# Layer 0 of a two-layer graph and expert kernel: chains of the third graph block over 12 groups, GpSimd's indirect DMAs in program order, first weights issued earlier

## The chip, the cores and the metric

The kernel runs on one core of one Trainium2 chip. Its time is the device time in microseconds of one execution; lower is better. Before the change three runs took 1025.27, 1031.23 and 1034.23 us (median 1031.23). Besides, one execution was recorded by the hardware profiler.

Engines are named as in the profile: PE (matrix multiply), PEld (its weight loads), DVE (vector), ACT (scalar, activation functions), POOL (GpSimd) and SP (here a queue that only issues DMAs). Every engine runs its own instructions in order. DMAs are issued by SP, by ACT and by POOL; an indirect DMA, which takes row numbers from a tile, is issued by POOL alone.

## The reference

Two layers, each a graph step and a mixture of experts, on 3327 rows of 256 numbers. The change is in layer 0:

```python
def _L0_gnn_ref(x, adj, W, b):
    a = (adj == 1).astype(x.dtype)
    deg = jnp.sum(a, axis=1, keepdims=True)
    agg = jnp.einsum('ij,jf->if', a, x) / deg
    return agg @ W.T + b

def _L0_ffn_ref(x, gate_w, gate_b, w1, w2, w3):            # 16 experts, hidden size 512
    logits = jnp.einsum('bsd,de->bse', x, gate_w) + gate_b
    probs = jax.nn.softmax(logits, axis=-1)
    top_probs, top_idx = jax.lax.top_k(probs, 2)
    ...
    hidden = jax.nn.silu(h1) * h2
    expert_out = jnp.einsum('bseh,eho->bseo', hidden, w3)
    return jnp.einsum('bseo,bse->bso', expert_out, dispatch)

x = x + _L0_gnn_ref(_layernorm(x, axis=-1), adj, L0_gnn_W, L0_gnn_b)
x = x + _L0_ffn_ref((_layernorm(x, axis=-1))[None], ...)[0]
```

Layer 1 is of the same build: attention over the graph, then two of six experts for each row.

## The kernel before

**Tiles and chunks.** The rows stand in 26 tiles of 128 (the last has 127). Four tiles make a chunk, 0 to 6; chunk 6 has two tiles.

**Graph step (`graph`).** The result rows are worked in three blocks: block 0 has chunks 0 to 2, block 1 chunk 3, block 2 chunks 4 to 6. In a block the matmuls (L797) run over groups of source tiles. For each group SP loads a piece of the transposed adjacency matrix (`load_adj`, L669 and, for the last rows, L672), DVE turns it into a mask (`mask_of`, L680 and L682), and PE multiplies. Adjacency tiles and masks have three buffers each (`AHEAD`). Block 0 and block 2 have 26 groups of one tile, block 1 has ten of up to three tiles. A group of block 2 is twelve matmuls.

**The chain of a chunk (`finish`).** When a block's sums are there, each of its chunks goes through a chain that is written as a generator of seven steps: the first two tiles' product with W (L740) and update of x (L743, L858); the other two; layer norm (`norm`, L263 to L275) with stores of x and of the normed rows to DRAM; transposes for the router (L757); logits (L825, L827); the first part of `dispatch`, which finds the two experts of each row up to the tile `took` (L297 to L327); the second part, which counts places with matmuls (L333 to L337), casts them to row numbers (`t_idx`, L359) and writes (row, source row, weight) into the experts' lists in DRAM: eight indirect DMAs a chunk, issued by POOL (L363). The chains of a block run beside the next block's groups, two chunks in turn. `left` counts the steps that remain, and `over` gives the number of groups over which they are spread: after a group of block b, `left` over (`over[b]` less the group's number) steps are taken, rounded up.

**Expert slots (`slots0`).** A slot is up to 256 places of one expert's list; 32 usual ones (0 to 31) are run, the first eight from the lists of chunks 0 to 3 alone. Slot s: SP loads its piece of the list (`places0`, tile `who`, L952); POOL gathers the normed rows by two indirect DMAs (`rows_in0`, tile `xg`, three buffers, L1002); PE transposes them (L1015); two halves of the hidden layer (`hidden0`, L1027, with L1031 on ACT and L1035 on DVE); the product with w3 (`out0`, L1050); the weighting on DVE (tile `y`, two buffers, L1055); and two indirect DMAs on POOL that add the rows to x in DRAM (L1056). The weights of an expert come by three loads on SP (`load0`, L978): w1 and w2 by `load0_hidden`, w3 by `load0_out`, into two sets of buffers. The texts call the DMAs of L1002 gather s, those of L1056 add s, and those of L363 list scatters.

**How they meet.** In block 2 `routed0` runs at group 21 and loads `who` for slots 0 to 7; it reads the lists and so waits until the scatters of chunks 0 to 3 have landed. At group 25 the first step of `slots0` runs (gathers 0 and 1, slot 0's weights and transposes). After the block, `beside` takes two steps of the chains of chunks 4 to 6 for each half slot. From slot 8 on, the places of a slot come from `rank_table` and the lists of all chunks.

**What sets the order.** A scheduler orders the instructions of each engine by what is ready, except where the program ties them: `tc.issue_after(x)` keeps an instruction behind x on its engine's queue. SP's loads of slots are tied by `in_order` and `last["who"]`; POOL's indirect DMAs of the slots are not tied to each other. `add_manual_dep` makes a real wait: in block 2's chunks each list scatter waits until the one two before it has landed.

Of the kernel before, what the change touches and what calls it, by code (L numbers as in the profile page):

```python
# [15 lines left out]
OP = mybir.AluOpType  # L16
# [3 lines left out]
P = 128  # L20
# [5 lines left out]
def kernel(  # L26
# [26 lines left out]
    nc = tc.nc  # L53
# [6 lines left out]
    NP = NT * P  # L60
# [35 lines left out]
    GRAPH0 = [CHUNKS[:3], CHUNKS[3:4], CHUNKS[4:]]  # L96
    NE0 = sum(map(len, CHUNKS[:4]))
    assert NE0 <= NF and len(GRAPH0[2]) <= 3
    SA = 2 * P
    HALF = E0 // 2  # L100
    WIDTHS = [SA, SA - 32, SA - 32, SA - 64, SA - 64, SA - 64, SA - 96, SA - 96]
    assert len(WIDTHS) == HALF and NP % SA == 0
    USUAL0 = 4 * HALF
# [14 lines left out]
    hd = dram.tile([NP, D], F32, name="hd")  # L118
# [4 lines left out]
    hd_of = dram_disjoint_views(hd[:, :], 2)  # L123
    xd = dram.tile([NP + SA, D], F32, name="xd")
    xd_of = dram_disjoint_views(xd[:, :], 5)
# [49 lines left out]
    for i in range(2):  # L175
        where = const.tile([P, NT, 2, 3], I32, name=f"where{i}")
# [64 lines left out]
    last = {}  # L241
# [37 lines left out]
    def dispatch(blk, logits, E, rows_of, seen, second_softmax):  # L279
# [3 lines left out]
        n, t0 = len(blk), blk[0]  # L283

        def col(name):
            return work.tile([P, BT], F32, name=name)[:, :n]

        def full(name):
            return work.tile([P, BT, E0], F32, name=name)[:, :n, :E]
# [5 lines left out]
        where = wheres[second_softmax]  # L295
        m, s, p = col("t_m"), col("t_s"), full("t_p")
# [56 lines left out]
        idx = work.tile([P, 2, BT], I32, name="t_idx")  # L353
# [6 lines left out]
        issued = []  # L360
        for j in range(n):
            for i in range(2):
                ins = nc.gpsimd.indirect_dma_start(  # L363
                    out=rows_of[2 * (t0 + j) + i],
                    out_offset=bass.IndirectOffsetOnAxis(ap=idx[:, i, j : j + 1], axis=0),
                    in_=where[:, t0 + j, i, :], in_offset=None, bounds_check=E * NP - 1, oob_is_err=False,
                )
                if len(issued) > 1 and (blk is GRAPH[1][-1] if second_softmax else blk in GRAPH0[2]):
                    tc.add_manual_dep(ins.ins, issued[-2], mybir.DependencyInfo(mybir.DependencyClass.Sync, mybir.DependencyReason.DATA))
                issued.append(ins.ins.name)  # L370
# [174 lines left out]
    @contextmanager  # L545
    def more(is_one, label):

        last.clear()
        with tc.If(is_one > 0, label=label, preferred_fallthrough_block=True):  # L549
            yield  # L550
        last.clear()

    def in_order():

        return tc.issue_after(last["who"].ins) if "who" in last else nullcontext()
# [30 lines left out]
    def bank(c, shape):  # L586

        return ps_c[c].tile(shape, F32, name=f"acc{c}") if c >= 0 else ps_mm.tile(shape, F32, name="mm")
# [23 lines left out]
    def weight(who, h):  # L612

        return who.bitcast(F32)[:, h, 2:3]
# [326 lines left out]
    def places0(s):  # L941

        run, table, row, col, _ = plan[s]
        who = io.tile([P, 2, 3], I32, name="who", bufs=16)
        if table is None:
            src = lists[0][run * NP : run * NP + SA, :]
        else:
            with in_order():
                at = nc.sync.value_load(early[table][row : row + 1, col : col + 1], min_val=0, max_val=E0 * NP)
            src = lists[0][bass.ds(at, SA), :]  # L950
        with in_order():
            last["who"] = nc.sync.dma_start(who, src.rearrange("(h p) w -> p h w", p=P))  # L952
        return who

    def routed0():

        for s in range(HALF):
            who[s] = places0(s)

# [17 lines left out]
    def load0(s, i, w):  # L977
        last["who"] = nc.sync.dma_start(w0[plan[s][0] % 2][i], w)  # L978

    def load0_hidden(s):  # L980
        run, table, row, _, _ = plan[s]
        if table is None:
            which[run] = slice(run, run + 1)
        else:
            with in_order():
                which[run] = bass.ds(nc.sync.value_load(early[table][row : row + 1, 0:1], min_val=0, max_val=E0 - 1), 1)
        with in_order():
            for i, w in enumerate((ffn0_w1, ffn0_w2)):
                load0(s, i, w[which[run]].rearrange("o (p k) h -> p (o k) h", k=KD))
# [5 lines left out]
    def parts0(s):  # L995
        n = plan[s][-1]
        return [(h, min(P, n - h * P)) for h in range(-(-n // P))]

    def rows_in0(s):
        xg = io.tile([P, 2, D], F32, name="xg", bufs=3)  # L1000
        for h, m in parts0(s):
            last["pool"] = nc.gpsimd.indirect_dma_start(  # L1002
                out=xg[:m, h, :], out_offset=None, in_=hd_of[0][: NE0 * P, :] if s < HALF else hd[:, :],
                in_offset=bass.IndirectOffsetOnAxis(ap=who[s][:m, h, 1:2], axis=0),
            )
        return xg

    def turned0(s, xg):
# [36 lines left out]
    def out0(s, hid):  # L1045
        w3 = w0[plan[s][0] % 2][2]
        ps = bank(2, [P, 2, D])
        for h, m in parts0(s):
            for c in range(NC0):
                nc.tensor.matmul(ps[:m, h, :], hid[c // 2][:, c % 2, h * P : h * P + m], w3[:, c // 2, c % 2, :],  # L1050
                                 start=(c == 0), stop=(c == NC0 - 1))
        y = io.tile([P, 2, D], F32, name="y", bufs=2)
        names = []
        for h, m in parts0(s):
            nc.vector.tensor_scalar(y[:m, h, :], ps[:m, h, :], weight(who[s], h)[:m, :], None, op0=OP.mult)  # L1055
            ins = nc.gpsimd.indirect_dma_start(  # L1056
                out=xd_of[2 + h] if s < USUAL0 else xd,
                out_offset=bass.IndirectOffsetOnAxis(ap=who[s][:m, h, 0:1], axis=0),
                in_=y[:m, h, :], in_offset=None, compute_op=OP.add,
            )  # L1060
            if s < USUAL0:
                waits(ins, [v for g, v in enumerate(x_added.get(s - 1, ())) if g != h])
                if s == 0:
                    waits(ins, x_stored[: len(GRAPH0[0]) + len(GRAPH0[1])])
                if s == HALF:
                    waits(ins, x_stored[len(GRAPH0[0]) + len(GRAPH0[1]) :])
                names.append(ins.ins.name)
        x_added[s] = names

    who = {}  # L1070
    xg, xT, hid, which = {}, {}, {}, {}

    def slots0(first, end):
        usual = not first
        for s in range(first - 3, end + 1):
            if usual and s in AHEAD_AT:
                graph1_ahead(AHEAD_AT.index(s))
            if usual and s == HALF - 3:
                early["rank"], *early["ranks"] = rank_table(seen0)
            if usual and s == HALF + 4:  # L1080
                early["spill"] = spill_table(*early["ranks"], seen_head)
            if usual and s == end - 2:
                early["more"] = asked(early["spill"], 0)
            if s == first - 1:
                load0_hidden(first)
            if first <= s < end and starts(s):
                if next_run(s) < end:
                    load0_hidden(next_run(s))
                load0_out(s)
            known = HALF if s < HALF - 3 else end  # L1090
            for i in range(max(who, default=-1) + 1, min(s + 4, known)):
                who[i] = places0(i)
            for i in range(max(xg, default=-1) + 1, min(s + 3, known)):
                xg[i] = rows_in0(i)
            if first <= s + 1 < end:
                xT[s + 1] = turned0(s + 1, xg[s + 1])
            if first <= s < end:
                hid[s] = [hidden0(s, xT[s], 0)]
                if usual:
                    head1(2 * (s - LATE0))  # L1100
                yield
            if first <= s - 1:
                out0(s - 1, hid.pop(s - 1))
            if first <= s < end:
                hid[s].append(hidden0(s, xT.pop(s), 1))
                if usual and s == end - 1:
                    spare = const.tile([P, 1], F32, name="spare")
                    nc.scalar.activation(spare, half[:, 0:1], AF.Exp, bias=hid[s][1][:, 0, 0:1], scale=0.0)
                if usual:
                    head1(2 * (s - LATE0) + 1)  # L1110
                yield
            elif s == first - 1:
                yield
# [61 lines left out]
    def beside(post):  # L1175

        for i, _ in enumerate(slots):
            for _ in range(3 if i == 0 else 2):
                if next(post, slots) is slots:
                    return  # L1180

    graph("0", GRAPH0, prepare0, 1.0, OP.is_equal, Later(0), update0, after0, 7, {(2, 21): routed0, (2, 25): lambda: next(slots)},
          (operands_early, derived, derived_late), over={1: 19, 2: 20}, finish_with=beside)

    graph1 = ctx.enter_context(ExitStack())
    pools1 = graph_pools("1", graph1)
# [80 lines left out]
    who = {}  # L1267
# [20 lines left out]
    xg, xT, h1, h2, zs = {}, {}, {}, {}, {}  # L1288
# [88 lines left out]
```

## Time and profile before

| | us |
|---|---|
| profiled execution, its own time | 1030.67 |
| its span, first to last instruction | 1028.9 |
| median of the three runs | 1031.23 |
| mean granted clock of PE in the span | 0.960 of full |
| block 2's first group on PE | 130.3 |
| block 2's last matmul ends | 222.30 |
| slot 31's last product on PE ends | 579.35 |

A line of the profile names the line of the kernel, the engine, the operation, and the tiles that it writes and reads (out<-in). In a timeline the first two numbers are the start and the length in us, xN is the number of instructions that were merged, and the brackets hold the idle time of that engine before the line and what ended it. In a table of waits the numbers are the total in us, how often, and the longest. "SPq" rows are DMAs that SP issues. Times given without more are us from the span's start.

### The profile page before, as it was taken

To read this page: it belongs to the slowest core of one execution; us is meant where nothing else is said; L and a number is where in the kernel's file an instruction comes from. 1 tells how busy PE (TensorE), PEld (TensorE's weight loads), DVE (VectorE), ACT (ScalarE), POOL (GpSimd) and SP (SyncE) were. 2 spreads that over 40 slices of the span, in tenths; PEclk is the share of its full clock that TensorE was granted. 3 is DMA by queue.
4 is the path that set the end of the run, shared out by engine and by line. 5 is a ranking of instruction groups with operands and counts; after the bars stand their busy time and mean duration, and the time that the engine had idled before them with its cause. 6 is when DMAs were issued, how large, how long until landed. Compare 5 with 4: busy or idle time off the path is not lost. (4 is left out here: it accounts for less than half of the span.)

```text
span 1028.9 us, 14333 instructions
## 1 busy us (share of the span) xinstructions
PE 929.3 (90%) x4505; PEld 782.0 (76%) x4505; DVE 497.6 (48%) x1824; ACT 260.8 (25%) x532; POOL 428.4 (42%) x408
## 2 busy tenths in 40 slices
PE   6889999859997999999999989999889588999980
PEld 5678888649886999888898777877668367888870
DVE  6565586225651222212223677658567442344663
ACT  3310302015321111111111443131132333444430
POOL 2040060632575345544544311005242476777741
PEclk9999999969998999999999999999999689999995
DMA  9989678457546575667788398867853955332375
GB/s 338 318 272 307 231 189 305 127 179 236 143 105 189 143 212 149 173 193 185 188 250 236 73 308 288 254 212 181 253 128 129 332 135 151 93 93 93 93 249 195
DMA packets 109634, 204.00 MB, mean 198 GB/s; under 512 B 31843, under 2 KB 64356, under 8 KB 109550
## 3 DMA queue, kind: packets, MB, share of 16 engines
q1 hardware_dynamic: 69952, 154.19, 47.3%
q0 software_dynamic: 20608, 30.69, 13.1%
q10 hardware_dynamic: 18990, 18.14, 5.9%
q8 instruction: 36, 0.59, 0.3%
q14 instruction: 48, 0.39, 0.1%
HBM read 173.74 MB, written 35.53 MB: 203 GB/s over the span
## 5 line engine op out<-in xcount | busy, mean ns | idle before, releaser
L797 PE MATMUL acc<-big,y 128*128 128x512 f32 (+2 forms) x1456 | 341.2, 389 | 28.3 <-DVE big L680 19.8
L797 PEld LDWEIGHTS acc<-big,y 128*128 128x128 f32 (+1 forms) x1456 | 264.3, 193 | 85.7 <-ACT y L853 9.2
L1027 PE MATMUL acc<-xT,w 128*128 128x256 f32 (+3 forms) x1024 | 212.8, 361 | 0.0
L1027 PEld LDWEIGHTS acc<-xT,w 128*128 128x128 f32 x1024 | 186.4, 198 | 15.9 <-issue 3.1
L363 POOL DMA_INDIRECT list<-where,t_idx x104 | 109.3, 1051 | 198.9 <-DVE t_idx L359 87.8
L680 DVE TENSOR_SCALAR big<-adj 128x1536 fp32r<-128x1536 int32 (+6 forms) x130 | 111.5, 860 | 121.3 <-DMA adj<-in_adj_t 78.2
L1056 POOL DMA_INDIRECT xd<-y,who x64 | 99.0, 1547 | 65.2 <-DVE y L1055 19.2
L1050 PE MATMUL acc<-w,hid 128*128 128x256 f32 (+3 forms) x512 | 118.0, 381 | 0.7 <-DVE x_out L439 0.7
L1002 POOL DMA_INDIRECT xg<-hd,who x64 | 63.2, 988 | 123.2 <-PE acc L1027 44.2
L1035 DVE TENSOR_TENSOR hid<-hid,acc 128x512 f32<-128x512 f32 (+3 forms) x64 | 40.1, 629 | 139.7 <-PE acc L1027 134.1
L1050 PEld LDWEIGHTS acc<-w,hid 128*128 128x128 f32 (+3 forms) x512 | 89.5, 178 | 20.7 <-issue 3.3
L1031 ACT ACTIVATE hid<-acc 128x512 f32<-128x512 f32 (+3 forms) x64 | 35.2, 550 | 202.6 <-PE acc L1027 195.9
L605 POOL DMA_INDIRECT zd<-y,who x58 | 70.2, 1210 | 25.2 <-DVE y L1264 14.3
L1250 ACT ACTIVATE h<-acc,v 128x256 f32<-128x256 f32 x116 | 55.0, 475 | 100.3 <-PE acc L1247 99.3
L580 POOL DMA_INDIRECT xg<-hd,who x58 | 57.9, 999 | 31.8 <-issue 15.8
L1247 PE MATMUL acc<-xT,v 128*128 128x256 f32 x232 | 63.5, 397 | 4.4 <-DMA v<-w1d 3.9
L1055 DVE TENSOR_SCALAR y<-acc,who 128x256 f32<-128x256 f32 x64 | 28.1, 478 | 71.7 <-PE acc L1050 68.0
L1262 DVE TENSOR_TENSOR y<-acc,v 128x512 f32<-128x512 f32 x29 | 20.1, 692 | 86.8 <-PE acc L1259 86.8
L1247 PE MATMUL acc<-h,v 128*128 128x256 f32 x232 | 61.3, 387 | 0.6 <-ACT h L1250 0.6
L268 POOL TENSOR_TENSOR ln_var<-ln_var,half 128x2 f32<-128x2 f32 (+2 forms) x19 | 15.2, 802 | 104.5 <-DVE ln_var L266 92.2
L1259 PE MATMUL acc<-v,h 128*128 128x256 f32 x232 | 56.7, 387 | 0.1
L1247 PEld LDWEIGHTS acc<-xT,v 128*128 128x128 f32 x232 | 44.6, 203 | 13.3 <-issue 4.2
(281 smaller groups left out, 926.7 us busy)
## 6 DMA issues: line engine op xcount, KB each, us to landing
adj<-in_adj_t SPq DMA_DIRECT2D x66, 768.0 KB, 6.4
w<-in_ffn_w SPq DMA_DIRECT2D x72, 512.0 KB, 5.8
adj<-in_adj_t SPq DMA_DIRECT2D x25, 639.5 KB, 6.0
adj<-in_adj_t SPq DMA_DIRECT2D x25, 512.0 KB, 4.3
v<-w1d SPq DMA_DIRECT2D x7, 898.0 KB, 10.5
hd<-ln_h ACTq DMA_DIRECT2D x12, 512.0 KB, 10.6
z<-zd SPq DMA_DIRECT2D x6, 1024.0 KB, 8.1
w_all<-w1d SPq DMA_DIRECT2D x6, 898.0 KB, 12.7
```

The lines of the kernel that those rows point to most:

```text
L363: ins = nc.gpsimd.indirect_dma_start(out=rows_of[2 * (t0 + j) + i], out_offset=bass.IndirectOffsetOnAxis(ap=idx[:, i, j : j + 1], axis=0), ...
L580: last["pool"] = nc.gpsimd.indirect_dma_start(out=xg[:, h, :], out_offset=None, in_=of, in_offset=bass.IndirectOffsetOnAxis(ap=who[:, h, 1 ...
L605: last["z"] = nc.gpsimd.indirect_dma_start(out=zviews[n * s + h], out_offset=bass.IndirectOffsetOnAxis(ap=who[:, h, 0:1], axis=0), in_=y[: ...
L680: last["mask"] = nc.vector.tensor_scalar(mask[:kr, :, :cols], a[:kr, :, :cols], value, None, op0=op)
L797: last["graph"] = nc.tensor.matmul(acc[c][k][:, :w], y[:kr, j, part, k * P : (k + 1) * P], mask[:kr, jj, i0 : i0 + w], start=(j == 0 and p ...
L1002: last["pool"] = nc.gpsimd.indirect_dma_start(out=xg[:m, h, :], out_offset=None, in_=hd_of[0][: NE0 * P, :] if s < HALF else hd[:, :], in_ ...
L1027: last["slot"] = nc.tensor.matmul(q[:, c, :n], w[:, k, h0 : h0 + 2 * P - 1 : 2], xT[:, k, :n], start=(k == 0), stop=(k == KD - 1))
L1050: nc.tensor.matmul(ps[:m, h, :], hid[c // 2][:, c % 2, h * P : h * P + m], w3[:, c // 2, c % 2, :], start=(c == 0), stop=(c == NC0 - 1))
L1056: ins = nc.gpsimd.indirect_dma_start(out=xd_of[2 + h] if s < USUAL0 else xd, out_offset=bass.IndirectOffsetOnAxis(ap=who[s][:m, h, 0:1], a ...
L1247: ins = nc.tensor.matmul(ps[:, c, :], w[:, k, c : H1 : NC1], src[:, k, :], start=(k == 0), stop=(k == 1))
L1250: last["act"] = nc.scalar.activation(dst[:, c, :], ps[:, c, :], AF.Relu, bias=w1s[s % 3][:, BB + 2 * i + c : BB + 2 * i + c + 1])
L1259: nc.tensor.matmul(ps[:, h, :], h2[:, c, h * P : (h + 1) * P], w[:, c, :], start=(c == 0), stop=(c == NC1 - 1))
```

## The change

It has three edits. The steps of the chains that are left in block 2 are spread over 12 groups and not 20. The gathers, the adds and, for the chunks of block 2, the list scatters are tied in the order in which the program names them: each is issued after the one before, by the new `in_turn_on_pool` and `last["pool"]`. `load0_hidden(0)`, the loads of w1 and w2 of slot 0, is called in `routed0` and no longer in `slots0`.

```diff
@@ dispatch
         for j in range(n):
             for i in range(2):
-                ins = nc.gpsimd.indirect_dma_start(
+                with in_turn_on_pool() if not second_softmax else nullcontext():
+                    ins = nc.gpsimd.indirect_dma_start(
...
+                if not second_softmax and blk in GRAPH0[2]:
+                    last["pool"] = ins
@@
+    def in_turn_on_pool():
+
+        return tc.issue_after(last["pool"].ins) if "pool" in last else nullcontext()
+
@@ routed0
+        load0_hidden(0)
         for s in range(HALF):
             who[s] = places0(s)
@@ rows_in0
-            last["pool"] = nc.gpsimd.indirect_dma_start(
+            with in_turn_on_pool():
+                last["pool"] = nc.gpsimd.indirect_dma_start(
...
@@ out0
-            ins = nc.gpsimd.indirect_dma_start(
+            with in_turn_on_pool():
+                ins = last["pool"] = nc.gpsimd.indirect_dma_start(
...
@@ slots0
-            if s == first - 1:
+            if s == first - 1 and first:
                 load0_hidden(first)
@@ graph("0", ...)
-          (operands_early, derived, derived_late), over={1: 19, 2: 20}, finish_with=beside)
+          (operands_early, derived, derived_late), over={1: 19, 2: 12}, finish_with=beside)
```

More of the change, by code (lines that the diff above doesn't have):

```diff
@@ L362, in dispatch @@
             for i in range(2):
[L363 to L367, printed above, removed]
+                with in_turn_on_pool() if not second_softmax else nullcontext():
+                    ins = nc.gpsimd.indirect_dma_start(
+                        out=rows_of[2 * (t0 + j) + i],
+                        out_offset=bass.IndirectOffsetOnAxis(ap=idx[:, i, j : j + 1], axis=0),
+                        in_=where[:, t0 + j, i, :], in_offset=None, bounds_check=E * NP - 1, oob_is_err=False,
+                    )
+                if not second_softmax and blk in GRAPH0[2]:
+                    last["pool"] = ins
                 if len(issued) > 1 and (blk is GRAPH[1][-1] if second_softmax else blk in GRAPH0[2]):
@@ L1001, in rows_in0 @@
         for h, m in parts0(s):
[L1002 to L1005, printed above, removed]
+            with in_turn_on_pool():
+                last["pool"] = nc.gpsimd.indirect_dma_start(
+                    out=xg[:m, h, :], out_offset=None, in_=hd_of[0][: NE0 * P, :] if s < HALF else hd[:, :],
+                    in_offset=bass.IndirectOffsetOnAxis(ap=who[s][:m, h, 1:2], axis=0),
+                )
         return xg
@@ L1055, in out0 @@
             nc.vector.tensor_scalar(y[:m, h, :], ps[:m, h, :], weight(who[s], h)[:m, :], None, op0=OP.mult)
-            ins = nc.gpsimd.indirect_dma_start(
[L1057 to L1060, printed above, removed]
+            with in_turn_on_pool():
+                ins = last["pool"] = nc.gpsimd.indirect_dma_start(
+                    out=xd_of[2 + h] if s < USUAL0 else xd,
+                    out_offset=bass.IndirectOffsetOnAxis(ap=who[s][:m, h, 0:1], axis=0),
+                    in_=y[:m, h, :], in_offset=None, compute_op=OP.add,
+                )
             if s < USUAL0:
```

## The prediction

> **What bounds the kernel now.** First the busy time by engine, then PE's waits in 200 to 340 us (the third graph block's end and the first expert slots), then the timelines of PE, SP and POOL there.
>
> ```profile
> PE 929.3 (90%) x4505; PEld 782.0 (76%) x4505; DVE 497.6 (48%) x1824; ACT 260.8 (25%) x532; POOL 428.4 (42%) x408
> ```
>
> PE is the bound, and only what makes it idle or slow moves the end. Its waits (total, times, longest):
>
> ```profile
> PE mm L1015 <- DMA xg<-hd,who: 16.6, 4, 8.2
> PE acc L797 <- DVE big L680: 4.9, 1, 4.9
> ```
>
> All of it is in two gaps, in PE's timeline (start, length, then idle before in brackets):
>
> ```profile
> 194.72 6.40 PE L797 MATMUL acc<-big,y 128*128 128x512 f32 x33
> 209.32 0.67 PE L1015 MATMUL mm<-ident,xg 128*128 128x128 f32 x2 [8.20 <-DMA xg<-hd,who]
> 212.05 0.70 PE L1015 MATMUL mm<-ident,xg 128*128 128x128 f32 x2 [2.06 <-DMA xg<-hd,who]
> 217.67 4.63 PE L797 MATMUL acc<-big,y 127*128 127x512 f32 x12 [4.91 <-DVE big L680]
> ...
> 277.58 0.63 PE L1015 MATMUL acc<-ident,xg 128*128 128x128 f32 x4
> ...
> 319.16 0.70 PE L1015 MATMUL mm<-ident,xg 128*128 128x128 f32 x2 [5.79 <-DMA xg<-hd,who]
> 320.41 0.70 PE L1015 MATMUL mm<-ident,xg 128*128 128x128 f32 x2 [0.55 <-DMA xg<-hd,who]
> 320.90 5.78 PE L1027 MATMUL acc<-xT,w 128*128 128x256 f32 x16
> ```
>
> Gap one: group 24 ends at 201.12 (the first line), slot 0's rows come late, the last mask group later still, and block 2 ends at 222.30. Gap two: slot 8's rows, 5.79 + 0.55 idle, and the next 16 matmuls take 5.78, not the usual 3.62: 8.5 us. Slot 5's transposes (277.58) wait for nothing. SP's queue shows what gap one hangs on:
>
> ```profile
> 180.85 7.62 SPq L669 DMA_DIRECT2D adj<-in_adj_t  x4
> 203.51 3.96 SPq L952 DMA_DIRECT2D who<-list  x8
> 207.59 0.88 SPq L978 DMA_DIRECT2D w<-in_ffn_w  x2
> ```
>
> SP stands still for 15 us at the first `who` load, which waits for the list scatters of chunks 0 to 3; all behind it waits too. POOL's timeline:
>
> ```profile
> 179.81 1.13 POOL L363 DMA_INDIRECT list<-where,t_idx  x1 [24.98 <-DVE t_idx L359]
> ...
> 201.31 0.97 POOL L363 DMA_INDIRECT list<-where,t_idx  x1 [0.30 <-issue]
> 206.18 1.00 POOL L1002 DMA_INDIRECT xg<-hd,who  x1 [3.89 <-DMA who<-list]
> ...
> 238.21 0.94 POOL L1002 DMA_INDIRECT xg<-hd,who  x1 [12.19 <-PE acc L1015]
> ...
> 268.43 1.01 POOL L363 DMA_INDIRECT list<-where,t_idx  x1 [0.30 <-issue]
> ```
>
> Sixteen scatters from 179.81, one every 1.4 us; the `who` load 23.7 us after their start. Slot 5's gather goes at 238.21, 30 us before chunk 4's eight scatters.
>
> **Chains over 12 groups.** 16 steps are left when block 2 starts (21 less 12, plus 7). They were taken one a group in groups 0 to 15; now two in each of groups 0 to 3, then one, to group 11. In the built program the position matmuls of chunks 2 and 3 (L333, L337) move from after 15 and 16 groups to 12.2 and 12.6. A group is 2.35 us (36 matmuls in 7.04 to 7.19 us), so chunk 2's come 2.8 x 2.35 = 6.6 sooner, at 170.7, and the scatters, 2.4 later as now, at 173.1. That is the best case. Against it: chunk 2's hT transposes move from after 9 groups to 5.6, and following DVE's rows (eight updates with statistics at 1.2 us, masks at 0.83, two norms at 2.5) its normed rows are ready some 2.3 us after PE asks (0 to 4). And in DVE's new order all 60-odd small operations of both dispatches stand between mask 12 and mask 13. Interleaved they step by 0.13 us: from logits to `took` 8.2 us (6.6 now, 167.01 to 173.61), while PE reaches L335 7.2 us after the logits: 1.0 late; mask 13 is 2.2 late as well, which delays PE but not the scatters. So the scatters start near 176 (173.1 to 179.8, the latter no gain), and the first `who` load goes at 199.7.
>
> **SP's order.** The built program puts the eight `who` loads after the 21st adjacency load of the block, ahead of groups 21 to 24; before, they stood after the 25th. PE ends group 20 at 201.12 - 4 x 2.31 = 191.9, or 197.4 with those 5.5 us of stalls, and stands: at the first half of slot 0's transposes, which now follow group 20, until 5.8 after the `who` load (203.51 to 209.32); then for group 21, whose load is issued 4.1 after it (eight issues), lands 4.1 to 6.0 later (range of these loads) and needs a 0.83 us mask: `who` + 10.5 = 210.2. Left are group 21 at the low clock (4.63, as at 217.67, where the granted clock was 0.50), four groups at 2.33 and 0.7 of transposes: 14.6. The block ends at 224.8, not 222.3; the first two matmuls after it, slow now (0.98), save 0.75. Net +1.75 (-2 to +6: the end moves one for one with the scatters' start).
>
> **First weights sooner.** 1 MB leaves 207.59 and is issued in block 1, after its seventh and eighth adjacency loads (92.8 to 101). The DMA share there is 0.85 in 95 to 100, then 0.53 and 0.26: cost nothing; uncovered it would be 1 MB at 330 GB/s, 3.2 us. It no longer stands before the last rows' load, but that load is now held by the `who` loads: no gain.
>
> **POOL in program order.** Before: gathers 4 and 5, add 0, gather 6, add 1, gather 7, chunk 4's and 5's scatters with add 2 between, add 3, chunk 6's, add 4, gather 8. Now: add 0, gather 4, add 1, chunk 4's eight, gather 5, chunk 5's eight, add 2, gather 6, add 3, chunk 6's four, gather 7, add 4, gather 8. Gather 5 queues behind indices ready at 267.2 (cast at 267.00). Eight scatters take 12.2 (268.43 to 280.62): the gather issues at 279.7 to 281.9 and lands 6.3 later, as the one at 238.21, which also met a slot's weight loads (these gathers: 2.6 to 7.6, median 3.0). Slot 5's transposes end at 287.7, not 278.2: 9.5 idle (4.5 to 10.5), and the low clock costs the 2.2 of gap two again: 11.7. Next: chunk 5's eight (10.9 without the adds between) to 293.1, add 2 to 297.0, gather 6 landed at 302, when PE asks (290.1 + 11.7). Chunk 6's positions stand behind the first of those transposes: indices at 304.5, four scatters in 5.6, gather 7 landed at 315.5, transposes ended at 316 against 302.0: 14 late, with 1.5 for the clock 15.5 (10 to 18). Gather 8 then issues behind add 4, near 318 to 320, and lands by 327; PE asks at 313.4 + 15.5 = 329. Gap two is gone: -8.5. Net +7 (+1.5 to +10).
>
> The Trainium skill (DMA: Bandwidth & Descriptors, Anatomy of one DMA) puts a GpSimd transfer at 2.0 us plus bytes over 436 GB/s. An estimate from it is 2.3 us for a 128 KB gather, so slot 5's stall would be 4 us less and the total about 4 less; the 6.34 row beside weight loads speaks against it.
>
> **Later slots.** Gather s+4 now waits for add s. From the end of a slot's L1050 to the transposes four slots on are 13.3 us (362.65 to 375.95), 11.8 at the shortest (486.21 to 497.98). In it must fit 0.9 (y), 3.5 (add), 0.3, 2.2 (gather) and a landing of 2.8 to 6.4: 9.7 to 13.3. Covered at most slots, at some of 24 to 31 not: +2 (0 to 8).
>
> **Sum** against the profiled execution's own time, 1030.67 (span 1028.9 and 1.8 around it; the median of the runs is 1031.23, 0.6 above): 1030.67 + 1.75 + 7 + 2 = 1041.4; I take 1042, as more of the bounds lie above than below.
>
> The Trainium skill (TensorE: Matmul & The Clock Gate, Part 1) gives a warm-up of some 3.4 us at half rate. An estimate from it is 1.7 us lost per long stall where I take 2.2 from gap two; with three stalls the sum would be 1 to 2 us lower.
>
> **Rivals.** (1) Faster: both gaps close. It decides at the list wave: landed before SP reaches the `who` loads (about 187, when mask 18 frees a buffer), nothing of the adjacency is held and the block ends at 201.1 + 1.4 + 2.3, near 205: -17, with the POOL chain at its low end, 1015; with the chain as reckoned, 1021 to 1023. It needs the scatters to start by 187 - 23.7 = 163; PE reaches their positions at 170.7 without any stall. 0.06. (2) Next to no change: scatters at 173, gathers landing in under 3 us, slot 5 late by 4.5: what gap two gives back pays for it, 1030 to 1037. For it: the median landing of 3.0. 0.30. (3) Worse: the later slots starve. If landings stay at 5 to 6.5, as for the gathers of slots 28 to 30, the margin of 11.8 to 13 is missed by 1 to 2 us in eight slots and now and then before: 8 to 16 more, 1050 to 1057. 0.14. (4) The forecast, 1037 to 1048: 0.50.
>
> **Numbers.** A measurement of this kernel tells 1% from no change, 10.3 us: bounds 1020.9 and 1041.5. Of (4) 0.38 lies above: slower 0.38 + 0.14 = 0.52; within, 0.12 + 0.30 = 0.42; faster 0.06. The range from 1031 to 1054 leaves out (1), the low end of (2) and the high end of (3).
>
> **What would show it.** Right: SP idle before `who` near 200 us with groups 21 to 24 behind it; PE idle from about 195 with the block ending past 221; a new PE wait at slot 5's transposes near 280 of over 4 us, one at slot 7's, and none at slot 8's. Wrong: block 2 ended by 215, slot 5 without a wait, or new waits in most slots after 9.

## The result and the profile after

The changed kernel takes 1042.43 us (median of four runs, 1038.71 to 1043.39) against 1030.14 for the kernel before on the same chip (1025.27 to 1034.23): a ratio of 1.0125, 95% interval 1.0083 to 1.0167. The profiled execution took 1043.39 (span 1041.6, mean granted clock of PE 0.952), 12.7 more than the one of before.

The first row of the page is busy time by engine. PE runs the same 4505 matmuls, but is busy for 8.2 us longer, at the lower clock, and idle for 4.5 us longer:

```profile
PE 937.5 (90%) x4505; PEld 786.5 (76%) x4505; DVE 496.4 (48%) x1824; ACT 260.3 (25%) x532; POOL 428.7 (41%) x408
```

PE's waits of 200 to 340 us in the changed kernel (total, times, longest):

```profile
PE acc L1024 <- DMA xg<-hd,who: 17.7, 2, 10.0
PE mm L1024 <- DMA xg<-hd,who: 5.8, 1, 5.8
PE acc L804 <- DVE big L689: 2.9, 1, 2.9
```

Before, the two gaps together were 16.6 + 4.9; now three places together are 17.7 + 5.8 + 2.9. PE's timeline of the changed kernel shows where (start, length, idle before in brackets):

```profile
203.38 0.67 PE L1024 MATMUL mm<-ident,xg 128*128 128x128 f32 x2 [5.76 <-DMA xg<-hd,who]
206.97 11.61 PE L804 MATMUL acc<-big,y 128*128 128x512 f32 x48 [2.92 <-DVE big L689]
...
218.58 2.55 PE L804 MATMUL acc<-big,y 127*128 127x512 f32 x12
...
286.29 1.10 PE L1024 MATMUL acc<-ident,xg 128*128 128x128 f32 x4 [9.95 <-DMA xg<-hd,who]
...
308.57 0.49 PE L1024 MATMUL acc<-ident,xg 128*128 128x128 f32 x1 [7.75 <-DMA xg<-hd,who]
...
322.26 0.63 PE L1024 MATMUL acc<-ident,xg 128*128 128x128 f32 x4
...
333.09 0.63 PE L1024 MATMUL mm<-ident,xg 128*128 128x128 f32 x4
```

Gap one has moved from behind group 24 to behind group 20 and is 8.7 instead of 15.2. Block 2 ends at 221.13 (222.30 before), but its first mask was also ready 1.1 sooner (124.20 for 125.30): the block itself is 96.9 long, as before (97.0). What the smaller gap gave went into a new stall ahead of it (2.08 for a mask at 177.30) and into the clock. The first row is of the windows of the kernel before, the second of the changed one (the fields behind the window and its length are busy times of PE, PEld, DVE, ACT and POOL, then the granted clock, the DMA share and GB/s):

```profile
160.00:174.00 14.00, 13.99 (x89) 12.31 (x88) 7.31 (x40) 2.29 (x6) 0.00 (x0) 1.00 0.96 368
160.00:174.00 14.00, 14.00 (x74) 11.88 (x72) 8.03 (x55) 1.48 (x4) 0.00 (x0) 0.76 0.58 225
```

The clock of this window was 1.00 before and PE ran 89 matmuls in it; now it is 0.76, and PE runs 74. From 174 to 186 it is 0.86 against 1.00. Slot 5 (286.29) now waits 9.95 and slot 6 (308.57) 7.75; slots 7 and 8 (322.26, 333.09) do not wait. POOL's timeline of the changed kernel, cut to the starts and ends of its stretches (L364 list scatters, L1011 gathers), gives the reason:

```profile
195.46 0.97 POOL L364 DMA_INDIRECT list<-where,t_idx  x1 [0.30 <-issue]
200.23 1.00 POOL L1011 DMA_INDIRECT xg<-hd,who  x1 [3.81 <-DMA who<-list]
...
265.71 1.02 POOL L364 DMA_INDIRECT list<-where,t_idx  x1 [1.56 <-DVE t_idx L359]
...
281.09 0.97 POOL L364 DMA_INDIRECT list<-where,t_idx  x1 [4.32 <-DMA list<-where,t_idx]
282.36 0.99 POOL L1011 DMA_INDIRECT xg<-hd,who  x1 [0.30 <-issue]
...
296.24 0.97 POOL L364 DMA_INDIRECT list<-where,t_idx  x1 [0.46 <-issue]
...
301.29 1.01 POOL L1011 DMA_INDIRECT xg<-hd,who  x1 [0.31 <-issue]
...
324.21 1.01 POOL L1011 DMA_INDIRECT xg<-hd,who  x1 [0.30 <-issue]
```

Gather 5 (282.36) leaves behind chunk 4's eighth scatter (281.09), 44 us later than before (238.21). Gather 6 (301.29) leaves behind chunk 5's eight and add 2. SP's queue in the changed kernel:

```profile
161.44 23.86 SPq L676 DMA_DIRECT2D adj<-in_adj_t  x7
197.65 3.96 SPq L959 DMA_DIRECT2D who<-list  x8
201.72 5.55 SPq L676 DMA_DIRECT2D adj<-in_adj_t  x4
```

SP stands until the last scatter (195.46) has landed, 2.2 later, and the loads of groups 21 to 24 stand behind it.

Where the 12.7 us arise is read from the ends of the slots' transposes, after against before: slot 4 -1.4, slot 5 +9.2, slot 6 +18.8, slot 7 +20.9, slot 8 +12.6, slot 9 +10.5, slot 31 +10.8. Another 1.9 come behind slot 31.

### The profile page after: what moved, and what is told of

Its sections match the earlier page's. It is cut to its first block, busy times and chain, and to the rows that moved or that the text cites. A ratio compares the mean times of both kernels' runs of the same rounds, so it can differ in the third digit from the quotient of the medians.

```text
span 1041.6 us, 14317 instructions
## 1 busy us (share of the span) xinstructions
PE 937.5 (90%) x4505; PEld 786.5 (76%) x4505; DVE 496.4 (48%) x1824; ACT 260.3 (25%) x532; POOL 428.7 (41%) x408
## 3 DMA queue, kind: packets, MB, share of 16 engines
q0 software_dynamic: 20608, 30.69, 12.7%
## 5 line engine op out<-in xcount | busy, mean ns | idle before, releaser
L804 PE MATMUL acc<-big,y 128*128 128x512 f32 (+2 forms) x1456 | 346.6, 392 | 25.8 <-DVE big L687 14.0
L364 POOL DMA_INDIRECT list<-where,t_idx x104 | 109.0, 1048 | 200.5 <-DVE t_idx L359 65.1
L1260 ACT ACTIVATE h<-acc,v 128x256 f32<-128x256 f32 x116 | 54.9, 473 | 100.4 <-PE acc L1257 99.4
L1011 POOL DMA_INDIRECT xg<-hd,who x64 | 62.6, 979 | 34.1 <-issue 17.7
L268 POOL TENSOR_TENSOR ln_var<-ln_var,half 128x2 f32<-128x2 f32 (+2 forms) x19 | 15.2, 802 | 101.0 <-DVE ln_var L266 89.6
L1257 PEld LDWEIGHTS acc<-xT,v 128*128 128x128 f32 x232 | 44.2, 201 | 12.2 <-issue 3.6
```

The source lines that it names most:

```text
L364: ins = nc.gpsimd.indirect_dma_start(out=rows_of[2 * (t0 + j) + i], out_offset=bass.IndirectOffsetOnAxis(ap=idx[:, i, j : j + 1], axis=0), ...
L804: last["graph"] = nc.tensor.matmul(acc[c][k][:, :w], y[:kr, j, part, k * P : (k + 1) * P], mask[:kr, jj, i0 : i0 + w], start=(j == 0 and p ...
L1011: last["pool"] = nc.gpsimd.indirect_dma_start(out=xg[:m, h, :], out_offset=None, in_=hd_of[0][: NE0 * P, :] if s < HALF else hd[:, :], in_ ...
L1257: ins = nc.tensor.matmul(ps[:, c, :], w[:, k, c : H1 : NC1], src[:, k, :], start=(k == 0), stop=(k == 1))
L1260: last["act"] = nc.scalar.activation(dst[:, c, :], ps[:, c, :], AF.Relu, bias=w1s[s % 3][:, BB + 2 * i + c : BB + 2 * i + c + 1])
```

## The experiments

The runs were taken in four sets (e1 to e4, e5 to e8, e9 and e10, e11 and e12), each on one chip beside its own runs of the kernel before, whose medians were 1036.67, 1036.84, 1051.26 and 1030.20; so ratios to before are compared, not times. A difference between two ratios carries both intervals, some 0.5 points (5 us). "Slot 4 to 9" is how much later slot 9's transposes end against before, less the same for slot 4: what is lost or won between them in the profiled execution, free of where block 2 began. "Block 2" is its length from the end of its first mask on DVE to its last matmul (97.0 before).

| run | ratio to before, 95% | block 2, us | slot 4 to 9, us |
|---|---|---|---|
| changed kernel | 1.0125 (1.0083 to 1.0167) | 96.9 | +11.9 |
| e1 order only | 1.0096 (1.0061 to 1.0130) | 97.7 | +13.4 |
| e2 chains only | 0.9997 (0.9973 to 1.0022) | 99.3 | -0.9 |
| e3 weights only | 0.9963 (0.9933 to 0.9993) | 93.5 | -0.5 |
| e4 list loads behind | 1.0071 (1.0040 to 1.0102) | 90.4 | +11.7 |
| e5 gathers ahead | 1.0065 (1.0038 to 1.0091) | 95.7 | +9.5 |
| e6 list scatters untied | 0.9991 (0.9962 to 1.0020) | 95.6 | +0.9 |
| e7 scatters unpaced | 0.9995 (0.9963 to 1.0027) | 95.4 | +4.0 |
| e8 list loads behind, free order | 0.9943 (0.9918 to 0.9967) | 92.8 | -0.9 |
| e9 as e8, unpaced | 1.0073 (1.0037 to 1.0110) | 96.9 | +7.3 |
| e10 e4 to e7 together | 1.0106 (1.0069 to 1.0144) | 100.4 | +8.6 |
| e11 as e9, pace of four | 0.9970 (0.9941 to 1.0000) | 89.9 | +2.8 |
| e12 e9 again | 0.9970 (0.9938 to 1.0002) | 92.0 | +2.9 |

The theory (A): the loss is slots 5 and 6, whose gathers stand behind list scatters on POOL; chains and weights gain next to nothing, because the list loads now hold groups 21 to 24 on SP. Rivals: the chains or the weights cost; or the order of gathers and adds costs by itself.

### The three parts alone

**e1, the order of POOL alone:** the changed kernel with

```diff
-          ... over={1: 19, 2: 12}, finish_with=beside)
+          ... over={1: 19, 2: 20}, finish_with=beside)
@@ routed0
-        load0_hidden(0)
@@ slots0
-            if s == first - 1 and first:
+            if s == first - 1:
```

> The change's GpSimd order alone, with the chains over 20 groups and the first weights where they were. Theory A (the loss is slots 5 and 6, whose gathers now stand behind chunk 4's and chunk 5's list scatters): stalls of 8 to 11 us at slot 5's transposes and 6 to 9 at slot 6's, no wait at slot 8's, the end of block 2 as before (222 +- 1.5), and 9 to 15 us over before: 1039 to 1045. Rival B (the chains or the weights carry the loss): within 4 us of before, 1026 to 1034.

PE's waits of 200 to 340 us in this run:

```profile
PE acc L1023 <- DMA xg<-hd,who: 18.4, 2, 10.9
PE mm L1023 <- DMA xg<-hd,who: 12.8, 2, 8.0
PE acc L804 <- DVE big L687: 4.3, 1, 4.3
```

The first line is slots 5 and 6 (10.87 and 7.53), the other two are gap one as before. The ratio is 1.0096, 10 us: the order alone makes most of the loss, and within the intervals all of it. Rival B falls.

**e2, the chains alone:** the kernel before with `over={1: 19, 2: 12}`.

> The chains over 12 groups alone. Theory A (sooner scatters gain nothing, because the list loads now stand ahead of the adjacency loads of groups 21 to 24 and hold them): the end of block 2 within 2.5 us of before, the total within 3 us of it, 1027 to 1033. Rival B (denser chains cost PE stalls that last to the end): 3 to 8 us slower. Rival C (the chains do close gap one): block 2 ends by 214, 8 us or more faster. In this one the first weights still stand between the list loads and the last rows' load, so the end of block 2 can be up to 1 us later than in the changed kernel.

PE's timeline in this run, gap one's two waits for masks:

```profile
209.19 11.13 PE L797 MATMUL acc<-big,y 128*128 128x512 f32 x48 [2.72 <-DVE big L682]
...
222.08 2.59 PE L797 MATMUL acc<-big,y 127*128 127x512 f32 x12 [1.52 <-DVE big L680]
```

The scatters did go sooner, but groups 21 to 24 wait (209.19) for the held loads, and the last group's load stands behind two weight loads, as before. Block 2 is 2.3 longer than before and ends 2.4 later, within the 2.5 expected; the time is the same.

**e3, the weights alone:** the kernel before with `load0_hidden(0)` in `routed0` and `if s == first - 1 and first`.

> The first weights sooner alone: 1 MB among the adjacency loads of block 1. Theory A: no visible cost in block 1, up to 1 us sooner at the last rows' load; within 2 us of before. Rival B (the transfer delays block 1's masks): block 1 ends 2 to 4 us later and the total is 2 to 4 us slower.

The ratio is 0.9963, 4 us, just clear of no change; more than the 2 expected, which its interval still holds. The wait for the last mask, 4.91 before, is 0.41 here:

```profile
216.81 3.86 PE L797 MATMUL acc<-big,y 127*128 127x512 f32 x12 [0.41 <-DVE big L680]
```

Block 2 is 3.5 shorter (slot 0's second half of rows waits 1.9 longer in return); of block 1, its first mask of block 2 comes 1.9 later than in before's profile, but the executions differ by as much among themselves (121.7 to 127.2 over all runs), so a cost there is not told apart. The one part that gains does so because the last rows' load loses 1 MB in front of it. The three ratios' departures add up to +0.56%, the whole change's is +1.25% (0.83 to 1.67); the intervals allow it, and in the whole change the weights' gain has no place, since that load is held by the list loads there.

### Gap one

**e4, the list loads behind the adjacency loads:** in the changed kernel `routed0` and the first step of the slots run after the last group's load has been issued:

```diff
-{(2, 21): routed0, (2, 25): lambda: next(slots)}
+{(2, 21): lambda: load0_hidden(0)}
...
+   behind={(2, 25): lambda: (routed0(), next(slots))}
@@ routed0
-        load0_hidden(0)
+        last["who"] = last["tail"]        # the last rows' adjacency load
```

> The changed kernel with the eight list loads of slots 0 to 7 moved behind all of block 2's adjacency loads on SP's queue (and slot 0's first step, its gathers and transposes, with them). Theory A (the list loads, held by the list scatters, hold groups 21 to 24): SP's adjacency loads end before 195, PE runs groups 21 to 24 without a wait of over 1 us, and at most 2 us of waiting is left for slot 0's rows; block 2 ends near 212 (221.1 in the changed kernel), so 7 to 11 us faster than the changed kernel, 1031 to 1036, with the stalls at slots 5 and 6 still there. Rival B (slot 0's rows hold the block's end anyway, or slots 0 to 4 wait instead): the end of block 2 moves by under 3 us, or the gain is given back by slot 4; 1039 to 1044.

PE's timeline in this run, the last of groups 21 to 24 and the last group:

```profile
197.74 4.90 PE L806 MATMUL acc<-big,y 128*128 128x512 f32 x24 [0.38 <-DVE big L689]
203.78 2.58 PE L806 MATMUL acc<-big,y 128*128 128x512 f32 x12 [1.15 <-DVE big L689]
208.67 0.48 PE L1026 MATMUL mm<-ident,xg 128*128 128x128 f32 x2 [2.30 <-DMA xg<-hd,who]
211.93 0.70 PE L1026 MATMUL mm<-ident,xg 128*128 128x128 f32 x2 [2.79 <-DMA xg<-hd,who]
212.28 3.78 PE L806 MATMUL acc<-big,y 127*128 127x512 f32 x12
```

PE runs to 206.4 with stops of 0.4 to 1.2, about as expected, then waits 5.1 for slot 0's rows, where at most 2 were expected. Block 2 ends at 216.06 (212 expected) and is 6.5 shorter than in the changed kernel, and the ratio fell by 0.54 points, 5.6 us, from 1.0125 to 1.0071, which is barely clear of both intervals. The stalls of slots 5 and 6 stay. The other profiles agree: chains over 12 groups with the list loads ahead give a block 2 of 95.4 to 99.3 (changed kernel, e2, e5, e6, e7), with the list loads behind 89.9 to 92.8 (e4, e8, e11, e12); only e9 and e10, in the set where before too was slow, have 96.9 and 100.4. The mechanism held, the size fell short of 7, for a reason that SP's and POOL's timelines show:

```profile
163.90 30.15 SPq L676 DMA_DIRECT2D adj<-in_adj_t  x11
197.71 0.81 SPq L679 DMA_DIRECT2D adj<-in_adj_t  x2
203.07 3.98 SPq L961 DMA_DIRECT2D who<-list  x8
```

```profile
194.12 0.98 POOL L364 DMA_INDIRECT list<-where,t_idx  x1 [0.30 <-issue]
205.72 1.00 POOL L1013 DMA_INDIRECT xg<-hd,who  x1 [10.62 <-DMA who<-list]
```

The last scatter was issued at 194.12, and the list loads could go 8.9 us after it, not 2.2. While SP stood still, the scatters had the DMA engines nearly to themselves (before, their share was 0.02 in 195 to 200 us); with the adjacency loads running, the median from issue to landing rose to 6.2 (4.9 in the changed kernel, 3.4 before), of those of the sixteen whose landing the trace shows (ten, ten and six). The Trainium skill (DMA: Bandwidth & Descriptors, Queues, rings and completion order) says that a DMA's semaphore write on an engine lands only after that engine's earlier writes, across its queues; late landings of small scatters beside large loads agree with it, but no run here separates this from plain sharing of the engines.

### Slots 5 and 6

**e5, gathers one slot further ahead:** the changed kernel with `min(s + 4, known)` for `min(s + 3, known)` in `slots0`'s loop over `rows_in0`. Gather 5 then stands ahead of chunk 4's scatters, gather 6 ahead of chunk 5's, gather 7 behind them.

> The changed kernel with each slot's gather one slot further ahead in program order, so that slot 5's stands ahead of chunk 4's list scatters and slot 6's ahead of chunk 5's. Theory A (the loss is the two gathers' places on GpSimd): no wait at slot 5's transposes, 0 to 2 us at slot 6's, 3 to 6 at slot 7's (behind chunk 5's scatters and add 2 now) and 0 to 4 at slot 8's; 8 to 14 us faster than the changed kernel, which is 6 us faster to 3 us slower than before. Rival B (the tie itself, every gather behind the adds of two or three slots before, is what costs): still 9 us or more slower than before.

PE's timeline in this run, slots 7 and 8:

```profile
305.93 0.67 PE L1024 MATMUL acc<-ident,xg 128*128 128x128 f32 x2 [7.57 <-DMA xg<-hd,who]
...
324.18 0.51 PE L1024 MATMUL mm<-ident,xg 128*128 128x128 f32 x2 [3.60 <-DMA xg<-hd,who]
326.31 0.70 PE L1024 MATMUL mm<-ident,xg 128*128 128x128 f32 x2 [1.63 <-DMA xg<-hd,who]
```

Slots 5 and 6 do not wait, as expected; but slot 7 waits 7.57 (3 to 6 expected) and slot 8 5.2. The gain is 0.6 points, 6 us, where 8 to 14 were expected. At 1.0065, 7 us slower than before, the time lies between theory A (up to 3 slower) and rival B (9 or more); that the waits left slots 5 and 6 speaks for A, and e6 decides it. The stall went to the next gather behind the scatters, and as PE came to slot 8 earlier, gap two was back.

**e6, list scatters untied:** the changed kernel without `in_turn_on_pool` and `last["pool"] = ins` at L364; gathers and adds keep their order. Gather 5 stands ahead of chunk 4's scatters, gather 6 behind the sixth of chunk 5.

> The changed kernel with the list scatters free of the order (gathers and adds keep theirs): slot 5's gather then stands ahead of chunk 4's scatters, slot 6's behind two thirds of chunk 5's. Theory A (it is the scatters): no wait at slot 5's, 7 to 10 at slot 6's, none at slots 7 and 8; from 2 us faster to 5 slower than before. Rival B (it is the order of gathers and adds): 9 us or more slower than before, with a wait at slot 5's.

PE's timeline, the only wait from 220 to 340:

```profile
298.94 0.49 PE L1022 MATMUL acc<-ident,xg 128*128 128x128 f32 x1 [8.60 <-DMA xg<-hd,who]
```

8.60 at slot 6, none at 5, 7 and 8, and the ratio is 0.9991: tying the scatters is what cost, and the order of gathers and adds by itself costs nothing that shows.

**e7, scatters unpaced:** the changed kernel without the wait of a block 2 scatter for the one two before it.

```diff
-                if len(issued) > 1 and (blk is GRAPH[1][-1] if second_softmax else blk in GRAPH0[2]):
+                if len(issued) > 1 and second_softmax and blk is GRAPH[1][-1]:
```

> The changed kernel without the rule that a list scatter of this block waits for the landing of the one two before it. Theory A (part of the delay is that wait: 16.35 us for eight scatters that take 1.28 each to issue): chunk 4's eight take 10 to 11 us, slot 5's wait is 4 to 6, slot 6's 2 to 5, and the kernel is 7 to 11 us faster than the changed one, 1 to 5 slower than before. Rival B (unpaced scatters are held elsewhere, at the queue, and the gather behind them lands later): within 3 us of the changed kernel.

POOL's timeline in this run, chunk 4's first and last scatter and gather 5:

```profile
266.73 1.02 POOL L364 DMA_INDIRECT list<-where,t_idx  x1 [1.57 <-DVE t_idx L359]
...
275.75 0.97 POOL L364 DMA_INDIRECT list<-where,t_idx  x1 [0.30 <-issue]
277.02 0.99 POOL L1011 DMA_INDIRECT xg<-hd,who  x1 [0.30 <-issue]
```

The eight take 10.0, not the 16.35 of the changed kernel. PE's timeline, the waits of slots 5 and 7:

```profile
283.71 0.67 PE L1024 MATMUL acc<-ident,xg 128*128 128x128 f32 x2 [6.36 <-DMA xg<-hd,who]
285.27 0.70 PE L1024 MATMUL acc<-ident,xg 128*128 128x128 f32 x2 [0.88 <-DMA xg<-hd,who]
...
313.83 0.50 PE L1024 MATMUL acc<-ident,xg 128*128 128x128 f32 x2 [1.58 <-DMA xg<-hd,who]
```

Slot 5 still waits 7.2 (4 to 6 expected), since gather 5 landed up to 6.9 after its issue and not 3.8 as in the changed kernel: that much of rival B came true. Slot 6 does not wait (2 to 5 expected), slot 7 waits 1.6. The ratio is 0.9995, 13 us better than the changed kernel (8 to 19 with both intervals; 7 to 11 expected); the profile shows 7.9 of it between slots 4 and 9, where 4.0 of the loss is left. So in the ratio either edit, e6 or e7, undoes the loss: it takes the tie and the scatters' wait for each other together.

### A version that beats both, and four more that did not

**e8:** the kernel before with chains over 12, weights sooner, the list loads behind as in e4, and POOL's order left to the scheduler.

> The kernel before with the chains over 12 groups and the first weights sooner, the list loads of slots 0 to 7 behind all of block 2's adjacency loads, and GpSimd's order left to the scheduler. Theory A (the two gaps are separate, and the list loads' place is what is worth having at gap one): block 2 ends near 214 to 216, gap two stays, 5 to 10 us faster than before. Rival B (the scatters, which in the run with the list loads behind landed up to 8.9 us after their issue beside the adjacency loads, take the gain back): within 3 us of before.

The ratio is 0.9943 (0.9918 to 0.9967), 6 us faster than before, and block 2 ends at 216.15, as theory A had it. How much of this the list loads' place adds is not shown: the first weights alone (e3) gave 0.9963 (0.9933 to 0.9993) and a block 2 of 93.5, against 92.8 here. Gap one shrinks, gap two stays, seen in PE's timeline at slot 0's halves and slot 8:

```profile
208.54 0.67 PE L1018 MATMUL mm<-ident,xg 128*128 128x128 f32 x2 [4.39 <-DMA xg<-hd,who]
211.97 0.70 PE L1018 MATMUL mm<-ident,xg 128*128 128x128 f32 x2 [2.76 <-DMA xg<-hd,who]
...
312.86 1.53 PE L1018 MATMUL mm<-ident,xg 128*128 128x128 f32 x4 [5.70 <-DMA xg<-hd,who]
```

**e9 and e10**, to shrink gap two: e9 is e8 with e7's edit; e10 is the changed kernel with the edits of e4 to e7 together.

> The run with the list loads behind and GpSimd's order free, now also without the rule that a list scatter waits for the landing of the one two before. Theory C (slot 8's gather can go only when the last list scatter of chunk 6 has landed and its list is loaded: in all runs so far its transposes end 13 to 20 us after that scatter's issue; the stretch of GpSimd's queue from chunk 4's first scatter to there is what sets gap two): chunk 6's last scatter is issued 4 to 7 us sooner (300.6 there), gap two shrinks from 5.7 to under 2.5, and the kernel is 3 to 8 us faster than that run, 9 to 14 faster than before. Rival (what holds chunk 6 is its own indices, or the scatters' landings lengthen as the queue fills): the last scatter within 2 us of 300.6 and the time within 2 us of that run.

> The changed kernel with four edits together: list loads behind the adjacency loads, list scatters untied and unpaced, gathers one slot further ahead. GpSimd then takes gathers 5 and 6 ahead of chunk 4's scatters, gather 7 behind add 2, gather 8 behind chunk 6's. Theory C: no wait at slots 5 and 6, 0 to 4 at slot 7's and 0 to 3 at slot 8's, the tied order of gathers and adds costing nothing in the later slots; 6 to 13 us faster than before. Rival (the tied order of gathers and adds costs by itself): 4 us or more slower than the run before this one, with waits at later slots.

Both forecasts missed: 1.0073 (1.0037 to 1.0110) and 1.0106 (1.0069 to 1.0144). In both, PE has a stretch that no other run shows; its timeline in e9:

```profile
286.27 0.58 PE L1030 MATMUL acc<-xT,w 128*128 128x256 f32 x1 [0.82 <-issue]
288.36 0.58 PE L1030 MATMUL acc<-xT,w 128*128 128x256 f32 x1 [1.50 <-issue]
290.46 1.01 PE L1030 MATMUL acc<-xT,w 128*128 128x256 f32 x2 [1.52 <-issue]
```

Sixteen matmuls that take 3.62 took 13.5 us (14.8 in e10), released by nothing that the profile shows, while POOL issued sixteen scatters in a row and the DMA engines moved 8 GB/s (276 to 292 us).

**e11 and e12**, to find whether the scatters in a row do this: e11 is e9 with a pace of four; e12 is e9 again.

```diff
-                if len(issued) > 1 and (blk is ...
-                    tc.add_manual_dep(ins.ins, issued[-2], ...
+                back = 2 if second_softmax else 4
+                if len(issued) >= back and (blk is ...
+                    tc.add_manual_dep(ins.ins, issued[-back], ...
```

> The run with the list loads behind, GpSimd's order free and the scatters unpaced, but now each of chunk 4's to 6's list scatters waits for the landing of the one four before it. GpSimd's order is the same as in the unpaced run. Theory D (with nothing to hold them, sixteen scatters in a row stall the other engines: in the two unpaced runs with sixteen in a row DVE stood 8 to 10 us and PE took its matmuls one by one from 280 to 294): no such stretch here, chunk 6's last scatter between 296 and 302, gap two under 5 us; 0.99 to 0.995 of before. Rival E (the stretch has nothing to do with the scatters, that chip was slow for all kernels then, before included): the stretch is here too, or in neither run of this call.

> The unpaced run once more, beside the one with a pace of four, on the same chip and against the same runs of before. Theory D: PE's matmuls one by one near 280 to 294 again, 1.004 to 1.011 of before. Rival E: no such stretch, and 0.985 to 0.993 of before, as reckoned for it first.

Both are at 0.997 (0.9941 to 1.0000 and 0.9938 to 1.0002), and neither has the stretch. So sixteen scatters in a row do not by themselves stop the engines; the same program had the stretch in one set and not in the other. In the set of e9 and e10 before too was slower (1051.26). What made the stretch stays open.

Without it, e12 still is not the 0.985 to 0.993 reckoned. In e11 chunk 6's last scatter left at 296.22, within the 296 to 302 expected, but slot 8 waited 9.4 us in both, where under 5 was expected for e11. PE's timeline in e12, slot 8's two halves:

```profile
314.18 0.70 PE L1018 MATMUL mm<-ident,xg 128*128 128x128 f32 x2 [4.85 <-DMA xg<-hd,who]
319.43 0.70 PE L1018 MATMUL mm<-ident,xg 128*128 128x128 f32 x2 [4.56 <-DMA xg<-hd,who]
```

Theory C's pace was not what bounds gap two: from the end of slot 4's transposes to the issue of chunk 6's last scatter it is 41.4 us before, 41.6 in e8 and 41.6 in e12. DVE's timeline in e12 names a nearer candidate:

```profile
294.42 0.43 DVE L393 TENSOR_TENSOR y<-k_key 128x256 f32<-128x256 f32 x1 [6.17 <-DMA xd<-y,who]
```

`rank_table` takes its scratch from the two buffers of `y`, so this instruction waits until add 2 has landed (the wait is 5.25 before, 5.68 in e8), and behind it on DVE stands the cast of chunk 6's last row numbers (L359, 294.76). But add 3, which stands ahead of chunk 6's scatters on POOL, left only at 295.10, though its rows `y` had been ready since 283.16: by the program each add waits until the one before has landed. Both ways lead back to add 2, whose second half was issued at 286.53 and landed at 294.32. A scratch of its own for L393 was not tried and would free only one of them, so what bounds gap two is read from the rows, not shown. Besides, the scheduler put add 4 between gather 8's halves in e11 and e12, which made the second wait.

## Why the prediction was right

The total (1042 for 1042.43; the sum 1041.4 for the profiled 1043.39) and the forecast's mechanism held: POOL's order makes new stalls behind the list scatters, the list loads hold groups 21 to 24, and gap two goes. Its terms are off by up to 5 us and cancel, so that the total is met to 0.4 us is luck.

- **Block 2's end.** Forecast +2.5; measured -1.2, of which 1.1 were there when the block began, so nothing. SP's idle time before `who` with groups 21 to 24 behind it is as forecast (197.65 for 199.7), and e4 shows it: with the list loads behind, the block is 6.5 shorter. Too large were the transposes' stall of chunk 2 (2.3 reckoned, 0.24 at L764; the mask's 2.2 was 2.08) and the way from `who` to group 21's mask (10.5 reckoned, 9.3 measured). PE ended group 20 at 197.62, as forecast (197.4), but for another reason in part: of the 5.5 us of stalls 2.3 came, and the clock of 0.76 in 160 to 174 us, which the forecast put at nothing, took most of the rest (14 us at 0.76 are 3.4 us lost).
- **Slot 5.** Forecast 9.5 idle and 2.2 for the clock; measured 9.95, and the sixteen matmuls behind it take 5.06 for 3.62, 1.4; behind slot 6's stall they take 5.88 for 3.74, 2.1. The 1.7 estimated from the Trainium skill (TensorE: Matmul & The Clock Gate, Part 1) lies between the two. The near hit of the idle time hides two errors: the scatters took 16.35 where 12.2 was reckoned, and gather 5 landed 3.8 after its issue where 6.3 was. e1 and e6 show that scatter order is the cause.
- **The second stall** was forecast at slot 7 (3.8 with the clock) with none at slot 6, and came at slot 6 (7.75). Three terms were mis-sized: "eight scatters take 12.2", which were 16.35, as two of them waited 2.66 and 4.32 for the landing of the one two before; chunk 5's eight, 12.3 for 10.9; and gather 6's landing, 7.3 after its issue, where 5 was reckoned. e7 takes the scatters' waits away: chunk 4's eight take 10.0, slot 6 does not wait, and slot 7 waits 1.6.
- **Gap two.** "Gap two is gone: -8.5": PE's wait is gone, and from slot 7 to slot 9 10.4 us came back. But the order did not close it. Gather 8 left at 324.21, 12 later than before (312.31, the row below); PE was only later still. e5, e8, e11 and e12 bring PE to slot 8 sooner and have the wait again.

```profile
312.31 1.01 POOL L1002 DMA_INDIRECT xg<-hd,who  x1 [0.79 <-PE acc L1027]
```

- **Middle, net.** From slot 4 to slot 9 it was +11.9, not +7, and outside the +1.5 to +10 given: up to slot 7 22.3 were lost (15.5 forecast, 10 to 18), and 10.4 came back (8.5).
- **Later slots.** Forecast +2 with rival 3 behind it; measured +0.3 from slot 9 to 31. There is no new PE wait in slots 10 to 31, though the landings that rival 3 asked for did come: from 340 us on the gathers landed 4.6 to 7.8 after their issue (median 6.7; before 2.7 to 6.4, median 2.9). Those that the trace shows were still there 0 to 2.8 before PE asked, so the margin held, but only just.
- **Weights.** No wait in block 1, as forecast; e3 shows a gain of 4 us alone, which has no place in the changed kernel, where the list loads hold the last rows' load.
- **Not in the forecast:** 1.9 behind slot 31, not followed up.

Slot 4 came 1.4 sooner where 1.75 later was reckoned (-3.15); the middle +4.9, the later slots -1.7 and what is behind slot 31 +1.9 add up with it to +1.95, the difference between the sum 1041.4 and the profiled 1043.39, but for rounding.

The Trainium skill's 2.3 us for a gather of 128 KB (DMA: Bandwidth & Descriptors, Anatomy of one DMA; an estimate) and the row of 6.3 that was taken lie on either side of gather 5, which landed in 3.8; gather 6 took 7.3. Neither serves for both.

## What to carry to other kernels

Tying a queue to program order moves every instruction behind what is long and late in it: list, for each DMA that feeds the bound engine, what stands ahead of it in the built queue, and price that work with its own waits, not at its issue rate. Before moving a load that waits, look at what is queued behind it, and keep waiting loads behind those that could run (e4). When a wait disappears, ask whether the resource came sooner or only the engine later: only the first is a gain that will last.

## What the runs showed of the hardware that was not expected

- The last three of the sixteen list scatters (128 rows of 12 bytes each) landed 2.1 to 2.2 us after their issue in the changed kernel, where SP stood and the DMA share was 0.14 (190 to 197 us), and up to 8.9 in e4, beside adjacency loads of 640 KB each: the standing load queue had kept them short.
- An eight-scatter stretch takes 10.0 us without waits (e7), 12.2 (before) to 16.35 (changed) when each waits for the landing of the one two before.
- In the changed kernel the granted clock fell to 0.76 in 160 to 174 us although PE was busy all that time and had not waited over 0.3 us in the 20 us before. In that window stand 32 router matmuls (L832, 16 columns each) nearly on end, as the denser chains put them. With chains over 12 groups the clock of this window was 0.76 in e2 too, 0.88 in e5, e6, e7, e8 and e12, and 1.00 in e4 and e11; with chains over 20 (before, e1, e3) it was 1.00. (e9 and e10 had a wait of 3.8 and 5.0 us shortly before.) So the drop goes with the denser chains but does not come in every execution; what decides it is not shown.
- In one set of runs two kernels had a stretch of 13.5 and 14.8 us in which PE took sixteen matmuls one by one (e9, e10); the program of e9 did not have it in another set (e12).
